# The projections of keys, values and queries on one 128x128 array or on four tiles of 128x32

## The chip, the core and the metric

The kernel runs on one core of a Trainium2 chip. The metric is the time of one execution on the device in microseconds (us), the median of several runs. A profile is of one execution, which has its own time.

## What is computed

The input is `x` of 16 images, 64x64 places, 128 features, all in 32-bit floating point. Layer 0 is a two-dimensional LSTM over each image (each place takes the states of the place above and to the left) after a group norm. Layer 1 is a Nystrom attention with 8 heads of 16 features and 64 landmarks, followed by a recurrent layer over the 4096 places. The change touches the attention alone, of which this is the core (b images, n = 4096 places, h = 8 heads, dh = 16, m = 64 landmarks):

```python
xn = (x - mu) * rsqrt(var + eps) * gamma + beta
q, k, v = split(xn @ w_qkv, 3)             # w_qkv is 128 x 384; then split into heads
q = q * dh ** -0.5
q_l, k_l = mean of q, k over each of the m landmarks' places
attn1 = softmax(q @ k_l.T)                 # n x m
attn2 = softmax(q_l @ k_l.T)               # m x m, then its pseudo-inverse, by 6 iterations
attn3 = softmax(q_l @ k.T)                 # m x n
out = attn1 @ pinv(attn2) @ (attn3 @ v) + convolution of v over 33 places
out = x + out @ w_out + b_out
```

## The kernel before

The program has five stages one after the other: statistics of the images, the LSTM over diagonals (`lstm_grid`), the landmarks with the pseudo-inverse (`landmarks`), the attention (`attention`, from line 845 on), and the recurrent layer (`recurrence`). In the trace the attention goes from some 1611 us to some 3370 us.

**Groups and steps.** The attention cuts the 4096 places of an image into Q = 8 groups of GC = 512 places, so 16 images are 128 groups. Groups go through a pipeline of two images' depth: in step s the group s is projected (`new`); the group s-8 of the image before (`mid`) has its attn3 exponentials and its sums over values; and the groups around s-16 of the image before that (`first`, `cur`, `third`, `fourth`, `fifth`, `sixth`) are finished: attn1, product with the inverse, convolution, output product, and the first product of the recurrent layer. Steps 0 to 7 run `first_step`, 8 to 14 `second_step`, 15 to 127 `step` (lines 1396 to 1484), and what is left `last_step`. A step with s a multiple of 8 has `start` set: the image changes, and between the projections and the next products stand extra ones that close the image before (`gather`, `turn_split`, `spread_values`). Of the 113 runs of `step`, 14 are such (s = 16, 24, ..., 120) and 99 are not.

**What sets the order.** The stage runs under a manual schedule: PE, DVE, ACT and POOL each execute in the order in which `step` calls its helpers; semaphores hold an instruction until its inputs are there and its buffer is free. SP issues the DMAs. PSUM holds eight banks of 128 partitions x 512 floats: `bank0` to `bank5`, and `pair`, which is two banks.

**The products around the change, in PE's order in a usual step.**

- `compare` (L1131): 16 products of 32 rows x 128 columns, four row tiles at a time, into banks 4, 5 and the pair.
- `project_keys` (L979): one product, weights `wqkv[:, 128:256]` (128x128), moving operand `xT` (128x512), into bank 0. ACT copies it to `KT` (L983).
- `project_values` (L989): four products, weights a 128x128 piece of `xT`, moving operand `wqkv[:, 256:384]` (128x128), into bank 1. ACT copies it to `V` (L993), and SP stores that.
- `project_queries` (L999): one product, weights `wqkv[:, 0:128]`, moving `xT`, into bank 5. ACT scales it into `QT` (L1003).
- `greatest` (L1024): four products of 32 rows x 128 columns x 512, into banks 0 to 3, so it needs the copies L983 and L993 done. DVE takes the maxima (L1028).
- `weigh` (L1054, L1060), `output` (L1208), `turn_top` (L1155), `turn_output` (L960 from `at_z`), `attend` (L1180: eight tiles of 64 rows x 32 columns side by side), `convolve` (L1103: the same tile), `feed` (L1240), `turn_rows` (L960 from `at_xh`), `attend_values` (L1076: four tiles of 128 rows x 32 columns side by side, 16 products of 128 columns), and `soften` (L1166, L1168).

A product in 32-bit floats stands in the trace as two passes, each a weight load (LDWEIGHTS, on the row PEld) and a MATMUL (row PE). A tile's rows are set by the partitions of the operands, its columns by the partitions of the output. `quarter(n)` is the slice of partitions 32n to 32n+32.

Of the kernel before, what the change touches and what calls it, by code (L numbers as in the profile page):

```python
# [14 lines left out]
P = 128  # L15
# [830 lines left out]
def attention(nc, tc, t1, gamma, beta, wqkv, ident, mhalf, fixed, xp, rows, qm, km, pinvT, vd, t2, wx, wx_stats, out, ahead):  # L846
# [16 lines left out]
    NP = H // 2  # L863
# [3 lines left out]
    with ExitStack() as ctx:  # L867
# [10 lines left out]
        def banks(*ks):  # L878
            return [bank(k, [P, GC]) for k in ks]
# [94 lines left out]
            gr.zT = wk.tile([P, GC], F32, tag="zT", name="at_zT")  # L974
            nc.scalar.copy(gr.zT, gr.pz)

        def project_keys(gr, p=None):
            gr.pk = banks(0)[0] if p is None else p
            nc.tensor.matmul(gr.pk, wqkv[:, P : 2 * P], gr.xT, start=True, stop=True)  # L979

        def keep_keys(gr):
            gr.KT = kv.tile([P, GC], F32, tag="KT", name="at_KT")
            nc.scalar.copy(gr.KT, gr.pk)  # L983

        def project_values(gr, p=None):
            gr.pv = banks(1)[0] if p is None else p
            for c in range(C):
                cs = slice(c * P, (c + 1) * P)
                nc.tensor.matmul(gr.pv[:, cs], gr.xT[:, cs], wqkv[:, 2 * P : 3 * P], start=True, stop=True)  # L989

        def keep_projected(gr):
            gr.V = kv.tile([P, C, F], F32, tag="V", name="at_v")
            nc.scalar.copy(gr.V.rearrange("p c f -> p (c f)"), gr.pv)  # L993
            rows = vd[gr.im.b, DH + gr.g * GC : DH + (gr.g + 1) * GC, :]
            nc.sync.dma_start(out=rows.rearrange("(k p) f -> p k f", p=P), in_=gr.V)

        def project_queries(gr):
            (gr.pq,) = banks(5)
            nc.tensor.matmul(gr.pq, wqkv[:, 0:P], gr.xT, start=True, stop=True)  # L999

        def keep_queries(gr):
            gr.QT = big.tile([P, GC], F32, tag="QT", name="at_QT", bufs=2 * Q + 1)
            nc.scalar.mul(gr.QT, gr.pq, 0.25)  # L1003

        def turn_split(im):
            r = bank(3, [P, P])
            nc.tensor.transpose(r, split.rearrange("p n s -> p (n s)"), ident)
            im.minus = wk.tile([P, P], BF, tag="minus", name="at_minus3")
            nc.scalar.copy(im.minus, r)
# [10 lines left out]
        def greatest(gr):  # L1020

            gr.s = banks(0, 1, 2, 3)
            for n in range(NP):
                nc.tensor.matmul(gr.s[n], gr.im.qm[quarter(n)], gr.KT[quarter(n)], start=True, stop=True)  # L1024
# [19 lines left out]
        def sums(im):  # L1044
            im.sums = sm.tile([P, P], F32, tag="sums", name="at_sums")
            im.total = wk.tile([P, NP, P], F32, tag="total", name="at_total", bufs=2)
# [24 lines left out]
        def attend_values(gr, k=5):  # L1071

            p = bank(k, [P, P])
            for c in range(C):
                for n in range(NP):
                    nc.tensor.matmul(  # L1076
                        p[quarter(n)], gr.V[:, c, quarter(n)], gr.e[:, n, c, :],
                        start=(c == 0), stop=(c == C - 1), skip_group_check=True,
                    )
            gr.p = p  # L1080

        def keep_values(gr):
            im, p = gr.im, gr.p
            if gr.g == 0:
                nc.vector.tensor_copy(im.sums, p)
            else:
                nc.vector.tensor_tensor(im.sums, p, im.sums, ALU.add)
# [37 lines left out]
        def compare(gr):  # L1125

            gr.both = pair()
            gr.s = (*banks(4, 5), gr.both[:, 0], gr.both[:, 1])
            for c in range(C):
                for n in range(NP):  # L1130
                    nc.tensor.matmul(  # L1131
                        gr.s[n][:, c * P : (c + 1) * P], gr.QT[quarter(n), c * P : (c + 1) * P],
                        gr.im.km[quarter(n)], start=True, stop=True,
                    )

        def topmost(gr):
            gr.mx = sm.tile([P, NP, C, 2], F32, tag="cmx", name="at_cmx")
            for s, n, k in ((gr.s[1], 1, 1), (gr.both.rearrange("p n x -> p (n x)"), 2, 2), (gr.s[0], 0, 1)):
                nc.vector.tensor_reduce(  # L1139
                    gr.mx[:, n : n + k].rearrange("p n c j -> p (n c j)"), s.rearrange("p (x m) -> p x m", m=M), AX.X, ALU.max  # L1140
                )
# [28 lines left out]
        def softened(gr):  # L1170
            gr.eT = wk.tile([P, NP, GC], F32, tag="eT", name="at_eT")
            for n in range(NP):
                nc.scalar.activation(gr.eT[:, n], gr.s[n], AF.Exp)  # L1173
# [42 lines left out]
        def measure(gr, cs=range(C)):  # L1216
            if 0 in cs:
                gr.mu = sm.tile([P, C, 2], F32, tag="mu", name="at_mu")
            for c in cs:
                st = sm.tile([P, 6], F32, tag="st", name="at_st")  # L1220
                nc.vector.bn_stats(st, gr.u[:, c, :])
                nc.vector.bn_aggr(gr.mu[:, c, :], st)
# [24 lines left out]
        def measure_feed(gr):  # L1247
            nc.vector.bn_stats(wx_stats[:, gr.im.b * Q + gr.g, :], gr.fx)
# [3 lines left out]
        def group(s):  # L1252
            b, g = divmod(s, Q)
            return images[b].groups[g] if b in images else None
# [141 lines left out]
        def step(s):  # L1396
            b, q = divmod(s, Q)
            new, after, mid, was = group(s), group(s + 1), group(s - Q), group(s - Q - 1)
            first, cur, third, fourth, fifth, sixth = (group(s - 2 * Q + d) for d in (1, 0, -1, -2, -3, -4))
            start = q == 0  # L1400
            if first:
                compare(first)
            if cur:
                softened(cur)
            project_keys(new)
            if start:
                sums(mid.im)
            project_values(new)
            if s == 2 * Q - 1:
                attend_values(was, 3)  # L1410
                keep_values(was)
            if first:
                topmost(first)
            if sixth:
                measure_feed(sixth)
            if fourth:
                measure(fourth, (0,))
            keep_keys(new)
            keep_projected(new)
            project_queries(new)  # L1420
            if start and was:
                gather(was.im)
            if fourth:
                measure(fourth, (1,))
            keep_queries(new)
            if start:
                turn_split(mid.im)
            if fifth:
                normalise(fifth)
            greatest(new)  # L1430
            if first:
                carry_factors(first)
                carry(first, 2, nc.gpsimd)
            weigh(mid)
            keep_greatest(new)
            if first:
                part_top(first)
            if third:
                output(third)
            weights(mid)  # L1440
            if first:
                carry(first, 3, nc.gpsimd)
            if start and was:
                spread_values(was.im)
            if first:
                turn_top(first)
            if fifth:
                turn_output(fifth)
                keep_output(fifth)
            if third:  # L1450
                keep_sum(third)
            if fourth:
                measure(fourth, (2, 3))
            if cur:
                attend(cur)
            if first:
                keep_top(first)
            add_weights(mid, (3, 1, 0), mid.g == 0)
            if fourth:
                factors(fourth)  # L1460
            add_weights(mid, (2,))
            if q == Q - 1:
                shift(new.im)
            if cur:
                convolve(cur, pair())
                divide(cur)
            if fifth:
                feed(fifth)
            if after:
                turn_rows(after)  # L1470
            if fifth:
                keep_feed(fifth)
            if after:
                keep_rows(after)
            if first:
                carry(first, 0, nc.scalar)
            attend_values(mid)
            if cur:
                add_convolved(cur)
            keep_values(mid)  # L1480
            if first:
                soften(first)
                carry(first, 1, nc.scalar)
                carry_bias(first)
            if cur:
                turn_attended(cur)
            fetch(s)
# [345 lines left out]
```

## Time and profile before

| what | value |
| --- | --- |
| time, median of 3 runs | 3641.82 us (3641.27 to 3644.77) |
| time of the profiled execution | 3638.97 us |
| its span, first to last instruction | 3637.4 us |
| mean granted TensorE clock | 0.991 |
| busy: PE, PEld, DVE, ACT, POOL | 96%, 65%, 82%, 69%, 68% of the span |
| instructions on PE and on PEld | 36874 each |
| a usual step (trace, 2401.41 to 2414.18) | 12.77 us |
| a step that changes the image (trace, 2452.65 to 2468.44) | 15.79 us |

The busy time of PE counts each MATMUL to its modelled end, and MATMULs overlap one another, so PE shows as busy where it only waits for the array to empty. What a product costs in the chain of PE is read from the distance between starts: from its first instruction's start to the start of the next line's.

### The profile page before, as it was taken

How to read it: one execution, taken by the hardware profiler on the slowest of the kernel's cores; microseconds unless marked ns; L12 is line 12 of the kernel's file. 1: busy time of each engine (PE TensorE's matmuls, PEld its weight loads, DVE VectorE, ACT ScalarE, POOL GpSimd, SP SyncE). 2: the span in 40 equal slices, each digit the busy share in tenths (PEclk: the TensorE clock that was granted, in tenths of full speed). 3: DMA queues.
4: the chain of work that ended last, by engine and by line, in shares of the span. 5: the costliest groups of instructions: out<-in, count | busy, mean ns of one | idle time of the engine just before them, and what ended most of it. 6: DMA issues, size and time to landing. Idle time of an engine off the chain costs nothing. (4 is left out here: it accounts for less than half of the span.)

```text
span 3637.4 us, 99065 instructions
## 1 busy us (share of the span) xinstructions
PE 3503.6 (96%) x36874; PEld 2372.5 (65%) x36874; DVE 2987.7 (82%) x7005; ACT 2499.6 (69%) x5126; POOL 2487.0 (68%) x3843
## 2 busy tenths in 40 slices
PE   7899999999999998999999999999999999997988
PEld 6666665545567666975666666666666666654777
DVE  8699999998889887544888888888888888888665
ACT  0466556666667666345788888888888888876787
POOL 1577877777788885325777777777777777785223
PEclk9999999999999999999999999999999999999999
DMA  9223332333333321033777777777676777667799
GB/s 349 76 75 79 81 84 81 83 83 86 87 86 85 80 77 36 4 74 85 165 174 186 166 165 164 163 167 163 161 162 162 162 166 164 157 143 187 199 273 183
DMA packets 834182, 484.04 MB, mean 133 GB/s; under 512 B 304672, under 2 KB 800672, under 8 KB 833696
## 3 DMA queue, kind: packets, MB, share of 16 engines
q1 hardware_dynamic: 814026, 442.55, 47.7%
q0 software_dynamic: 17728, 34.61, 5.3%
q8 instruction: 294, 4.82, 0.6%
q14 instruction: 192, 1.57, 0.1%
q10 hardware_dynamic: 1942, 0.50, 0.1%
HBM read 239.21 MB, written 238.29 MB: 131 GB/s over the span
## 5 line engine op out<-in xcount | busy, mean ns | idle before, releaser
L1096 POOL TENSOR_TENSOR at_total<-at_total,at_e 128x512 f32<-128x512 f32 x472 | 601.4, 1274 | 238.1 <-ACT at_e L1069 218.5
L290 ACT ACTIVATE ls_g<-ls_z,ls_b 128x304 f32<-128x304 f32 (+26 forms) x950 | 493.4, 545 | 222.8 <-PE ls_z L288 190.8
L283 PE MATMUL ls_z<-ls_xn,ls_w 128*128 128x432 f32 (+28 forms) x1700 | 587.4, 493 | 1.5 <-POOL ls_xn L275 1.2
L283 PEld LDWEIGHTS ls_z<-ls_xn,ls_w 128*128 128x128 f32 x1700 | 310.6, 191 | 189.6 <-issue 98.9
L288 PE MATMUL ls_z<-ls_hsum,ls_u 128*128 128x304 f32 (+26 forms) x1140 | 367.9, 459 | 0.0
L1028 DVE TENSOR_REDUCE at_mxq<-at_bank 128x1 f32<-128x512 f32 x512 | 317.7, 682 | 52.8 <-PE at_bank L1024 52.8
L323 POOL TENSOR_TENSOR ls_tt<-ls_ve,mhalf 128x8 f32<-128x8 f32 (+2 forms) x190 | 312.8, 1646 | 18.3 <-DVE ls_ve L322 2.0
L288 PEld LDWEIGHTS ls_z<-ls_hsum,ls_u 128*128 128x128 f32 x1140 | 210.1, 192 | 128.3 <-issue 78.3
L1173 ACT ACTIVATE at_eT<-at_bank 128x512 f32<-128x512 f32 x512 | 264.3, 603 | 41.4 <-PE at_bank L1168 40.8
L406 ACT ACTIVATE ls_g<-ls_cell 128x304 f32<-128x304 f32 (+26 forms) x190 | 93.2, 491 | 268.4 <-DVE ls_cell L405 268.4
L288 PE MATMUL ls_z<-ls_h,ls_u 128*128 128x304 f32 (+26 forms) x760 | 255.4, 459 | 12.3 <-DVE ls_h L410 12.3
L402 POOL TENSOR_TENSOR ls_g<-ls_g,ls_cell 128x304 f32<-128x304 f32 (+26 forms) x190 | 180.4, 949 | 126.6 <-ACT ls_g L290 115.8
L340 ACT ACTIVATE ls_tt<-ls_tt,ls_nb 128x128 f32<-128x128 f32 (+9 forms) x632 | 261.0, 478 | 4.3 <-POOL ls_tt L323 3.4
L275 POOL TENSOR_TENSOR ls_xn<-ls_xn,grstd 128x272 f32<-128x272 f32 (+40 forms) x186 | 209.8, 1128 | 75.1 <-DVE ls_xn L270 66.7
L1139 DVE TENSOR_REDUCE at_cmx<-at_bank 128x8 f32<-128x512 f32 x256 | 175.5, 685 | 104.0 <-PE at_pair L1131 102.4
L1244 ACT COPY at_fx<-at_bank 128x512 f32<-128x512 f32 x128 | 134.1, 1048 | 143.6 <-PE at_bank L1240 138.0
L1615 DVE SCALAR_TENSOR_TENSOR rc_y<-rc_w,rc_scale,rc_z 128x256 f32<-128x256 f32 x344 | 154.5, 480 | 86.2 <-PE rc_z L1602 84.4
L1234 ACT ACTIVATE at_z<-at_u,at_nb,at_r 128x128 f32<-128x128 f32 x512 | 209.6, 484 | 4.6 <-POOL at_nb L1229 4.5
L288 PEld LDWEIGHTS ls_z<-ls_h,ls_u 128*128 128x128 f32 x760 | 141.1, 191 | 106.8 <-issue 52.5
L1596 POOL DMA_DIRECT2D out_dram<-rc_tt x64 | 77.4, 1209 | 168.2 <-ACT rc_tt L1593 147.8
L1189 DVE STREAM_TRANSPOSE at_t<-at_bank 128x512 f32<-128x512 f32 x256 | 167.9, 694 | 28.4 <-PE at_bank L1180 27.3
L1602 PE MATMUL rc_z<-rc_y,rc_vT 128*128 128x256 f32 x688 | 172.9, 392 | 12.5 <-ACT rc_y L1623 11.8
(283 smaller groups left out, 9809.6 us busy)
## 6 DMA issues: line engine op xcount, KB each, us to landing
at_win<-vd SPq DMA_DIRECT2D x256, 256.0 KB
t<-ls_tt SPq DMA_DIRECT2D x392, 130.0 KB
at_T<-t SPq DMA_DIRECT2D x128, 264.0 KB
gs_xb<-in_x_dram SPq DMA_DIRECT2D x64, 512.0 KB
at_xh<-t SPq DMA_DIRECT2D x128, 256.0 KB
vd<-at_v SPq DMA_DIRECT2D x128, 256.0 KB
t<-at_u SPq DMA_DIRECT2D x128, 256.0 KB
out_dram<-at_u SPq DMA_DIRECT2D x128, 256.0 KB
```

Source lines behind the costliest of these rows:

```text
L275: eng.tensor_tensor(a, a, norm(v, grstd), ALU.mult)
L283: nc.tensor.matmul(v.z[g][:, : v.total], wt[g], v.xn[:, : v.total], start=True, stop=True)
L288: nc.tensor.matmul(view(v, v.first.z[g]), ut[g], hin, start=False, stop=True, skip_group_check=True)
L290: nc.scalar.activation(a[:, : v.cols], z, AF.Tanh if g == 4 else AF.Sigmoid, bias=bt[g])
L323: nc.gpsimd.tensor_tensor(v.tt[:, 0:k, F + 2 : F + 4], ve[:, :, :k].rearrange("p r k -> p k r"), mhalf[:, : 2 * k].rearrange("p (k r) -> p ...
L340: nc.scalar.activation(v.tt[:q, k, F + 4 :], v.tt[:q, k, 0:F], AF.Identity, bias=v.nb[:q, k : k + 1], scale=v.tt[:q, k, F + 3 : F + 4],)
L402: nc.gpsimd.tensor_mul(v.a[1], v.a[1], v.cl)
L1028: nc.vector.tensor_reduce(gr.im.mxq[:, n : n + 1, gr.g], gr.s[n], AX.X, ALU.max)
L1096: eng.tensor_tensor(total, total, e[:, :, c, :], ALU.add)
L1139: nc.vector.tensor_reduce(gr.mx[:, n : n + k].rearrange("p n c j -> p (n c j)"), s.rearrange("p (x m) -> p x m", m=M), AX.X, ALU.max)
L1173: nc.scalar.activation(gr.eT[:, n], gr.s[n], AF.Exp)
L1234: nc.scalar.activation(gr.z[:, c, :], gr.u[:, c, :], AF.Identity, bias=gr.nb[:, c : c + 1], scale=gr.r3[:, c : c + 1])
```

## The change

The projections of keys, values and queries get a flag `apart`. With it a product is no longer one of 128 weight columns but four of 32 columns, each into its own quarter of the output's partitions, with the same moving operand. The operands, the banks, the results and the places in the order stay what they are. `step` sets the flag unless the step changes the image; `first_step` and `second_step` do not set it.

```diff
+        def product(out, lhsT, rhs, apart):
+            for r in map(quarter, range(NP)) if apart else (slice(0, P),):
+                nc.tensor.matmul(out[r], lhsT[:, r], rhs, start=True, stop=True)
+
-        def project_keys(gr, p=None):
+        def project_keys(gr, p=None, apart=False):
             gr.pk = banks(0)[0] if p is None else p
-            nc.tensor.matmul(gr.pk, wqkv[:, P : 2 * P], gr.xT, start=True, stop=True)
+            product(gr.pk, wqkv[:, P : 2 * P], gr.xT, apart)
...
-        def project_values(gr, p=None):
+        def project_values(gr, p=None, apart=False):
             gr.pv = banks(1)[0] if p is None else p
             for c in range(C):
                 cs = slice(c * P, (c + 1) * P)
-                nc.tensor.matmul(gr.pv[:, cs], gr.xT[:, cs], wqkv[:, 2 * P : 3 * P], start=True, stop=True)
+                product(gr.pv[:, cs], gr.xT[:, cs], wqkv[:, 2 * P : 3 * P], apart)
...
-        def project_queries(gr):
+        def project_queries(gr, apart=False):
             (gr.pq,) = banks(5)
-            nc.tensor.matmul(gr.pq, wqkv[:, 0:P], gr.xT, start=True, stop=True)
+            product(gr.pq, wqkv[:, 0:P], gr.xT, apart)
...
-            project_keys(new)
+            project_keys(new, apart=not start)
             if start:
                 sums(mid.im)
-            project_values(new)
+            project_values(new, apart=not start)
...
-            project_queries(new)
+            project_queries(new, apart=not start)
```

(`NP` is 4, `P` is 128.) The last three edits are in `step`.

## Prediction

> **What bounds the kernel now.** I read the page first: PE is busy nearly throughout, its clock is granted in full, and every other engine has room.
>
> ```profile
> PE 3503.6 (96%) x36874; PEld 2372.5 (65%) x36874; DVE 2987.7 (82%) x7005; ACT 2499.6 (69%) x5126; POOL 2487.0 (68%) x3843
> ...
> PEclk9999999999999999999999999999999999999999
> ```
>
> A busy PE can still be a waiting PE, so I next took the timeline of PE over one step that is no change of image, from one L979 to the next. Columns: start, length, line, tile (rows*columns), shape, count.
>
> ```profile
> 2401.41 1.13 PE L979 MATMUL at_bank<-at_xT,wqkv 128*128 128x512 f32 x2
> 2402.37 1.05 PE L989 MATMUL at_bank<-wqkv,at_xT 128*128 128x128 f32 x8
> 2403.26 1.02 PE L999 MATMUL at_bank<-at_xT,wqkv 128*128 128x512 f32 x2
> 2404.22 1.14 PE L1024 MATMUL at_bank<-at_KT,qm 32*128 32x512 f32 x8
> ...
> 2408.15 1.09 PE L1180 MATMUL at_bank<-at_eT,at_g 64*32 64x512 f32 x16
> 2409.04 0.64 PE L1103 MATMUL at_pair<-at_win,bands 64*32 64x256 f32 x16
> 2409.60 1.13 PE L1240 MATMUL at_bank<-at_zT,at_wfT 128*128 128x512 f32 x2
> 2410.57 0.60 PE L960 MATMUL at_bank<-ident,at_xh 128*128 128x128 f32 x4
> 2411.10 1.08 PE L1076 MATMUL at_bank<-at_e,at_v 128*32 128x128 f32 x32
> 2412.11 0.40 PE L1166 MATMUL at_bank<-at_topT,at_minus 32*128 32x512 bf16 x4
> ```
>
> Only distances between starts count here. L989 needs 0.89 us for its eight passes of 128 columns. L979 needs 0.96 for two passes of 512 columns, and so does L1240 (0.97): both come straight after another tile shape. L1180 also makes two rounds of 512 columns straight after another shape, but in tiles of 32 columns, and needs 0.89.
>
> Single records of the trace (to the ns, medians of the 98 usual steps s = 17 to 127) tell why. Write E for the first weight load of L979. After the last MATMUL of another shape starts, the next shape's first load comes 0.200 later where that MATMUL has 128 columns: 0.107 for its own streaming and 0.093 in which the array empties. This 0.093 is the same in each direction (L1131 to L979, L960 to L1076, L1076 to L1166, L1060 to L1208). Then the first pass lasts longer than the others, since its weight load has nothing to hide under: L979's first pass takes 0.533 and its second 0.429, so 0.104 of load is bare. With 32 columns the bare load is small: L1180's first round takes 0.454 and its second 0.429; L1076's first 0.134, each later one 0.109. So 0.025 is bare.
>
> Usual steps repeat at 12.77 (12.77 to 12.78 in most, up to 12.93), so one chain sets them. Adding the streaming of a step's 17 groups (107 ns for each 128 columns of a round in f32, 53 in bf16) gives about 11.3; seven changes of shape at some 0.12 to 0.20 and a few ns per pass make the rest. So **PE's own order bounds these steps**, and a piece taken off its chain shortens them.
>
> **The change, part by part.**
>
> *Keys.* Two passes become two rounds of four tiles. In L1076 and L1180 the tiles of a round start 6.7 ns apart (0, 7, 14, 20) and both passes interleave by rounds, so I price a round as they show it: first 0.454, second 0.429, against 0.533 and 0.429. Gain 0.079.
>
> *Values.* Eight passes at 0.1113 on average (0.779 from the first to the last start, 0.112 to L999) become eight rounds at 0.1092, L1076's pace: 0.891 against 0.874. Gain 0.017.
>
> *Queries.* First round 0.429 against 0.431. The last pass now ends with the fourth tile, 0.020 after the first, so the way to L1024's load is 0.020 + 0.427 + 0.093 = 0.540 against 0.521. Loss 0.017. L1024's own first load of 128 columns stays bare as before.
>
> Sum: 2.805 before (0.533 + 0.429 + 0.779 + 0.112 + 0.431 + 0.521), 2.726 after: **0.079 a step**, 0.075 if the array empties as slowly as L1076 to the first MATMUL of L1166 has it (0.205). That saving is a load of 128 columns at the change of shape becoming one of 32; nothing streams faster.
>
> The Trainium skill (TensorE: Matmul & The Clock Gate, LDWEIGHTS) gives a load as its columns over 1.2 GHz, 107 ns for 128 and 27 for 32. The trace's 104 and 25 agree; by the page the sum would be 0.080.
>
> *Instructions.* Six products become 24, so 36 more pairs of load and MATMUL, on 190 in a step. In a round of L1076 four pairs go out in 20 ns, so PE's sequencer can issue them; I take them at nothing beyond the 20 ns above. If that cover is gone, see the second rival.
>
> *Waits.* The change adds none; it lets PE arrive 0.08 earlier, so I looked at what is next in time.
>
> Two rows of the waits (us in total, times, longest):
>
> ```profile
> DVE at_cmx L1139 <- PE at_pair L1131: 102.4, 112, 1.8
> ...
> PEld at_bank L1024 <- ACT at_v L993: 84.8, 112, 0.8
> ```
>
> The second is 0.757 each time and looks like a bound, but the copy L993 ends at E+2.64 and the load goes at E+2.81, just when the array is empty; L993 itself waits for L989, which moves ahead with the rest. The keys' copy L983 is held by ACT (the four L1173 end at E+1.33), so it will not move; it still ends 0.9 before L1024. By the first row DVE starts each step with 0.9 idle, waiting for L1131; then runs without a stop to L1203. It gains little until L1028 (ready some 0.03 before PE's L1024 ends), so DVE will lag PE by up to 0.05 after that. The closest demand on it is bank 5 for L1131: L1087 ends at 2412.83, the load goes at 2412.88, the MATMUL at 2413.195, so the last of its four tiles' loads (2412.896 + 0.107) leaves 0.19, then 0.14. POOL waits 1.87 per step for the exponentials (L1069), which follow PE. No DMA moves in order; the queues carry the same bytes in a step that is 0.6% shorter, at 77% busy in the step above.
>
> *Which steps.* `step` runs 99 times without `start`. In s = 15 PE waits 1.34 before L999 for bank 5, so its gain is lost there; I count 98. In steps that change the image L1007 comes right when POOL has the split ready (L1042 ends 2456.34, load 2456.40); that chain starts from L1069 of the step before, behind the projections, and moves with PE. So all 98 hold: 98 x 0.079 = **7.7 us** (7.4 at 0.075). The profiled execution would take 3638.97 - 7.7 = 3631.3. The runs' median lies 2.85 above that execution; from it, 3641.82 - 7.7 = **3634.1**, 0.21% less. What a measurement of this kernel can tell from no change is about 0.2%, or 7.3 us, so the forecast sits on that line.
>
> **Rivals.**
>
> 1. *A round is dearer because all four tiles read one operand* (slower). In L1076, L1180 and L1131 the tiles of a round stream different data: other columns of `at_e` or `at_eT`, or other partitions. Here four tiles stream the same `xT`, or the same columns of `wqkv`, at the same time, and no row shows that. If the reads stand in each other's way, the 12 rounds' worth of 2.56 us streaming grows; the change loses from 3.1% on (0.079 / 2.56). Two by two would double it: (2.56 - 0.08) x 98 = 243, so 3885 us. For it: nothing but the missing row. Against: the tiles of a round start 6.7 ns apart and read eight streams at once in L1180 without slowing. Chance 0.08.
>
> 2. *Starts cost more than 6.7 ns.* With 25 ns between the tiles of a round, the fourth ends 0.075 after the first instead of 0.020, rounds of 128 columns still hide it (4 x 25 = 100 under 109), and a step gains 0.079 - 0.055 = 0.024: 2.4 us, 3639.5. Against: 6.7 ns in four groups of the step. The Trainium skill (TensorEngine Tiling, Instruction Overhead) gives every matmul some 60 cycles, which is 25 ns at the full clock, and by it this rival would hold; the trace's rows of tiles side by side do not bear it out. Together with other partial losses (a bare load of the next tile, DVE's margin of 0.14 used up): chance 0.10, at 3637 to 3641.
>
> 3. *Hidden anyway*: another engine holds the step at 12.77. For it: the regular length, and DVE's long run. Against: DVE's idle 0.9, POOL's 1.87, and PE's distances, which the shapes alone explain. 3641.8, chance 0.06.
>
> That the change does not do what it says is excluded: the built program has four rows of 32x512 for L979 and 16 of 32x128 for the values in these steps.
>
> **How the numbers follow.** Forecast 0.74, rival 1 0.08, rival 2 0.10, rival 3 0.06, and 0.02 for more than forecast. Within the forecast the medians can differ by 1 to 2 us by chance, and 7.7 is 0.4 beyond the line, so I give 0.44 of its 0.74 to faster and 0.30 to no change. Faster 0.46, same 0.30 + 0.10 + 0.06 - 0.01 = 0.45, slower 0.08 + 0.01 (chance) = 0.09. The range goes from 3631 (the profiled execution's own base) to 3642 (rival 3): it leaves out rival 1 and the tail.
>
> **What would show it.** Right: the distance from L979's first start to L1024's falls from 2.81 to 2.73, L979's first round is 0.454, the values' rounds are 0.109 apart, usual steps repeat at 12.69, steps that change the image stay at 15.79. Wrong: rounds over 0.43 or 0.11 (rival 1), tiles of a round more than 7 ns apart (rival 2), a new idle in front of L1024, L1131 or L1208 with steps still at 12.77 (rival 3), or a longer emptying of the array between L1131 and the keys than 0.093.

## The result, and the profile after

The changed kernel takes 3635.2 us, the median of 22 runs (3628.9 to 3640.0), against 3642.2 us of the kernel before (22 runs beside them, 3636.5 to 3647.3). The ratio is 0.9979, with a 95% interval of 0.9973 to 0.9985, which is 5.5 to 9.8 us less.

In the changed kernel the lines behind the new helper stand 4 further down, and all three projections are recorded at the helper's line, L979. L1024 of before is L1028, L1131 is L1135, and so on. The page first:

```profile
span 3636.9 us, 106193 instructions
...
PE 3499.9 (96%) x40438; PEld 2343.7 (64%) x40438; DVE 2982.8 (82%) x7005; ACT 2499.9 (69%) x5126; POOL 2489.2 (68%) x3843
...
PEclk9999999999999999999999999999999999999999
```

The page has 3564 more MATMULs (36 a step in 99 steps: 18 products more, of two passes each), nearly the same shares, and a span only 0.5 us shorter than before's. The page can't show the gain, so I took the timeline of PE over one usual step (start, length, line, tile, shape, count):

```profile
2406.92 1.06 PE L979 MATMUL at_bank<-at_xT,wqkv 128*32 128x512 f32 x8
2407.80 1.06 PE L979 MATMUL at_bank<-wqkv,at_xT 128*32 128x128 f32 x32
2408.68 1.04 PE L979 MATMUL at_bank<-at_xT,wqkv 128*32 128x512 f32 x8
2409.65 1.14 PE L1028 MATMUL at_bank<-at_KT,qm 32*128 32x512 f32 x8
```

Keys now take 0.88 from start to start instead of 0.96, values 0.88 instead of 0.89, queries 0.97 instead of 0.96. From the first start of the keys to L1028 it is 2.73 where it was 2.81. The windows of two steps in a row, cut at the first start of the keys (columns: window, length, busy time of PE, PEld, DVE, ACT and POOL with counts, granted clock, DMA share, GB/s), show that the whole step keeps this gain:

```profile
2406.92:2419.61 12.69, 12.69 (x226) 8.15 (x222) 11.32 (x24) 10.66 (x22) 10.10 (x17) 1.00 0.75 170
2419.61:2432.30 12.69, 12.69 (x226) 8.23 (x222) 11.32 (x24) 10.63 (x22) 10.10 (x17) 1.00 0.72 167
```

The single records, as medians over the 98 usual steps (us; "to L1028" is L1024 before):

| | before | after | predicted |
| --- | --- | --- | --- |
| last start of L1131 (L1135 after) to the keys' first start | 0.200 | 0.200 | 0.200 |
| keys, first round | 0.533 | 0.453 | 0.454 |
| keys, second round, to the values | 0.429 | 0.429 | 0.429 |
| values, first start to that of the queries | 0.891 | 0.873 | 0.874 |
| queries, first round | 0.431 | 0.429 | 0.429 |
| queries, first to fourth tile's start | 0 | 0.020 | 0.020 |
| last start to L1028's load | 0.521 | 0.521 | 0.520 |
| keys' start to L1028's load | 2.805 | 2.726 | 2.726 |
| a usual step | 12.774 | 12.694 | 12.69 |
| eight steps, one change of image among them | 105.208 | 104.653 | |

Eight steps lose 0.555, which is seven times 0.079: the eighth, where the image changes, lost nothing. From L1028 of step 17 to that of step 127 the stretch is 7.45 us shorter (1436.82 against 1444.27). Three usual steps in it gained nothing: those that begin at L1028 of s = 41, 45 and 49 last 12.93 in both kernels. In them DVE starts its maxima (L1032) some 0.35 later than in step 42, and PE stands longer in front of L1212 than there, by 0.15 (by 0.07 in front of L1208 before).

**Why the span hides it.** In these two profiled executions the stages ahead of the attention, whose code is the same, took 6.7 us longer after than before (the first L1028 came at 1622.5 against 1615.8), and steps 14 to 17 took 40.79 against 38.74. In both places the clock record has stretches at half clock. The windows around step 15 in the profile of after (column before the DMA share: granted clock):

```profile
1705.00:1715.00 10.00, 8.11 (x120) 5.77 (x112) 1.76 (x3) 2.65 (x5) 6.93 (x8) 0.66 0.07 19
1715.00:1735.00 20.00, 16.49 (x250) 11.42 (x246) 11.11 (x20) 11.68 (x24) 12.07 (x26) 1.00 0.17 48
1735.00:1739.00 4.00, 4.00 (x68) 2.28 (x52) 2.96 (x5) 1.50 (x4) 2.90 (x3) 0.57 0.21 49
```

PE idles 1.9 us of the first window, 1.4 and 0.5 just ahead of 1708.2 while it waits for the exponentials (L1073); from 1707.9 to 1714.8 the clock is granted at half, and again for most of the third window. Before had one such piece there, from 1701.6 to 1705.0. The whole span had 75.5 us at half clock after, and 65.3 before. The seventh experiment, further down, has the same step 15 and one short piece there, so the changed code of that step does not by itself make the stretch longer. One execution's whole time says little about a change of 8 us; the distances inside the steps, all at full clock, say it to some ns.

### The profile page after: what moved, and what is told of

Its sections match the earlier page's. It is cut to its first block, busy times and chain, and to the rows that moved or that the text cites. A ratio compares the mean times of both kernels' runs of the same rounds, so it can differ in the third digit from the quotient of the medians.

```text
span 3636.9 us, 106193 instructions
## 1 busy us (share of the span) xinstructions
PE 3499.9 (96%) x40438; PEld 2343.7 (64%) x40438; DVE 2982.8 (82%) x7005; ACT 2499.9 (69%) x5126; POOL 2489.2 (68%) x3843
## 5 line engine op out<-in xcount | busy, mean ns | idle before, releaser
L1032 DVE TENSOR_REDUCE at_mxq<-at_bank 128x1 f32<-128x512 f32 x512 | 314.9, 677 | 53.0 <-PE at_bank L1028 53.0
L979 PE MATMUL at_bank<-at_xT,wqkv 128*32 128x512 f32 (+1 forms) x1684 | 262.8, 602 | 2.0 <-DVE at_cmx L1143 1.1
```

Source lines behind the costliest of these rows:

```text
L979: nc.tensor.matmul(out[r], lhsT[:, r], rhs, start=True, stop=True)
L1032: nc.vector.tensor_reduce(gr.im.mxq[:, n : n + 1, gr.g], gr.s[n], AX.X, ALU.max)
```

## The experiments

The theory: the time saved in a usual step is the keys' first weight load, bare at the change of tile shape, which has 32 columns instead of 128; the price is the skew of the four tiles at the end. The rivals: (a) the tiles stream faster or overlap more than one product does, so that each projection saves something by itself; (b) only the keys matter, and the other two could stay as they were; and, for the order of the tiles, that it does not matter in which order their passes are written. All edits are made on the changed kernel.

**Experiments 1 and 2: keys alone, and keys with values.** The rest goes back to one product of 128 columns.

```diff
 # experiment 1
-            project_values(new, apart=not start)
+            project_values(new)
...
-            project_queries(new, apart=not start)
+            project_queries(new)
 # experiment 2: only the second of these
```

> Only the keys are four tiles; values and queries are whole again. Theory (each change of tile shape costs the emptying of the array, 0.093 us, plus a bare weight load, 0.104 for 128 columns and 0.025 for 32; nothing else changes): against the kernel before, the keys gain 0.079, and a new change of shape in front of the values costs 0.020 + 0.093 + 0.104 - 0.002 = 0.215, so a usual step is 0.136 longer, 12.91 us, and the run 13.3 us longer (ratio 1.0037). Rival a (the tiles themselves make a product cheaper, each product keeps its own share): the step is shorter than before, 12.69 to 12.75. Rival b (it is the earlier copy of the keys on ACT that helps): the same gain as the full change, 12.69.

> Keys and values are four tiles, queries whole. Theory: against before the keys gain 0.079, the values 0.015, and the change of shape now stands in front of the queries: 0.020 + 0.093 + 0.104 more there. A usual step is 0.118 to 0.122 longer, 12.89 us, the run some 11.7 us longer (ratio 1.0032). Rival a: 12.68 to 12.70, nearly the whole gain of the change, since the values are the largest part. Rival b: 12.69.

Measured: 3652.97 us for keys alone, ratio to the kernel before 1.0035 (1.0023 to 1.0047), and 3652.08 us for keys and values, 1.0029 (1.0020 to 1.0038). Usual steps repeat at 12.913 and 12.893, as expected. The timelines, keys alone first:

```profile
2408.82 1.07 PE L979 MATMUL at_bank<-at_xT,wqkv 128*32 128x512 f32 x8
2409.82 1.16 PE L979 MATMUL at_bank<-wqkv,at_xT 128*128 128x128 f32 x8
2410.81 1.02 PE L979 MATMUL at_bank<-at_xT,wqkv 128*128 128x512 f32 x2
2411.76 1.14 PE L1028 MATMUL at_bank<-at_KT,qm 32*128 32x512 f32 x8
```

```profile
2410.25 1.06 PE L979 MATMUL at_bank<-at_xT,wqkv 128*32 128x512 f32 x8
2411.13 1.06 PE L979 MATMUL at_bank<-wqkv,at_xT 128*32 128x128 f32 x32
2412.12 1.12 PE L979 MATMUL at_bank<-at_xT,wqkv 128*128 128x512 f32 x2
2413.18 1.14 PE L1028 MATMUL at_bank<-at_KT,qm 32*128 32x512 f32 x8
```

With keys alone the way from the keys to the values is 1.00 (0.88 in the full change) and that of the values 0.99, of which the single records put 0.104 on the values' first round: the bare load of 128 columns has moved from the keys to the values. With keys and values it has moved on to the queries: 0.99 from the values to them, and their first round is 0.533. In each, a new change of shape costs what the old one cost (emptying plus bare load), and the keys' round is still the 0.453 of the full change. So rivals (a) and (b) fall: no projection gains more for itself than the 0.018 of the values' rounds, and of the sets of projections that were run only the whole of what stands between one change of shape and the next makes the step shorter.

**Experiment 3: two tiles of 64 columns.**

```diff
-            for r in map(quarter, range(NP)) if apart else (slice(0, P),):
+            for r in map(half, range(2)) if apart else (slice(0, P),):
```

> Two tiles of 64 columns in place of four of 32 in the same steps. Theory (the bare load goes with the columns): about half of 0.104 stays bare, 0.052; first round 0.481 in place of 0.533; the values' rounds at some 0.110; the skew at the end 0.007. A usual step is 0.059 shorter than before, 12.715 us, the run 5.8 us shorter (ratio 0.9984). Rival c (what matters is that the tile is the one that other products of the step use, 32 columns): no gain, 12.77. Rival d (any split takes the whole load away): 12.69.

Measured: 3636.55 us, ratio 0.9988 (0.9979 to 0.9997); usual steps at 12.707.

```profile
2401.79 1.08 PE L979 MATMUL at_bank<-at_xT,wqkv 128*64 128x512 f32 x4
2402.70 1.04 PE L979 MATMUL at_bank<-wqkv,at_xT 128*64 128x128 f32 x16
2403.57 1.03 PE L979 MATMUL at_bank<-at_xT,wqkv 128*64 128x512 f32 x4
2404.53 1.14 PE L1028 MATMUL at_bank<-at_KT,qm 32*128 32x512 f32 x8
```

The keys' first round is 0.480, so the bare load is 0.051: 0.104, 0.051 and 0.025 for 128, 64 and 32 columns, in proportion. The skew is 0.007 instead of 0.020. The step gained 0.067 where 0.059 was expected: I had put the values' rounds halfway, and they take 0.109, as with 32 columns. The theory holds in size as well as in sign.

**Experiment 4: the passes of the values written tile by tile.** Same products; all four pieces of `xT` for the first quarter of columns, then for the second, and so on.

```diff
-            for c in range(C):
-                cs = slice(c * P, (c + 1) * P)
-                product(gr.pv[:, cs], gr.xT[:, cs], wqkv[:, 2 * P : 3 * P], apart)
+            for r in map(quarter, range(NP)) if apart else (slice(0, P),):
+                for c in range(C):
+                    x = gr.xT[:, c * P : (c + 1) * P]
+                    nc.tensor.matmul(
+                        gr.pv[r, c * P : (c + 1) * P], x[:, r], wqkv[:, 2 * P : 3 * P], start=True, stop=True
+                    )
```

> As the change, but the values' 16 products are written tile by tile: the four pieces of one tile one after the other, then the next tile, so neighbours in PE's order use the same tile. Theory (PE starts its passes in the order written, and only neighbours on different tiles overlap): the values lose their rounds, up to 32 passes of 0.107 us = 3.4 us in place of 0.87, at best some overlap where tiles meet; a usual step of 15 us, up to 250 us more in all. Rival e (PE finds passes for free tiles by itself, whatever the order): 12.69 us a step as in the change.

Measured: 3768.56 us in one run; a step 14.073, that is 1.38 more than in the change. The values are L994 here, L1031 is the L1028 of the change.

```profile
2422.05 1.06 PE L979 MATMUL at_bank<-at_xT,wqkv 128*32 128x512 f32 x8
2422.93 2.11 PE L994 MATMUL at_bank<-wqkv,at_xT 128*32 128x128 f32 x29
2424.78 0.63 PE L979 MATMUL at_bank<-at_xT,wqkv 128*32 128x512 f32 x3
2424.88 0.49 PE L994 MATMUL at_bank<-wqkv,at_xT 128*32 128x128 f32 x3
2425.21 1.02 PE L979 MATMUL at_bank<-at_xT,wqkv 128*32 128x512 f32 x5
2426.16 1.14 PE L1031 MATMUL at_bank<-at_KT,qm 32*128 32x512 f32 x8
```

The order does matter, but my expectation of up to 15 was for tiles strictly one after the other, and they are not. A tile has eight passes; the single records show the next tile's first pass beginning as the fifth of the tile before it begins (2423.371 and 2423.377). So about two tiles run at any time, and the queries' first tiles (third row) start before the values' last tile is done. The expectation had room for some overlap where tiles meet, but neither side of it had two tiles running beside one another all along.

**Experiment 5: the values in pairs of pieces.** Now a tile has four passes in a row before the next tile's are written.

```diff
-            for c in range(C):
-                cs = slice(c * P, (c + 1) * P)
-                product(gr.pv[:, cs], gr.xT[:, cs], wqkv[:, 2 * P : 3 * P], apart)
+            for c0 in range(0, C, 2):
+                for r in map(quarter, range(NP)) if apart else (slice(0, P),):
+                    for c in (c0, c0 + 1):
+                        x = gr.xT[:, c * P : (c + 1) * P]
+                        nc.tensor.matmul(
+                            gr.pv[r, c * P : (c + 1) * P], x[:, r], wqkv[:, 2 * P : 3 * P], start=True, stop=True
+                        )
```

> As e4, but a tile gets only two neighbouring products (four passes) before the next tile's. In e4 the next tile began when the fifth of a tile's eight passes began, so I now hold that PE hands passes out in the order written, each tile taking one that runs and three that wait. By that, four passes of a tile all fit, the next tile starts some 7 ns later, and a usual step is 12.69 us again. Rival (only direct neighbours on different tiles overlap): half of e4's loss or so stays, 13.1 to 13.5 us. Rival (room for fewer waiting passes): 12.8 to 13.4 us.

Measured: 3645.46 us in one run (3646.04 for the kernel before beside it); a step 12.747, 0.053 more than in the change. The values are L995 here, and L1032 is the L1028 of the change.

```profile
2419.55 1.06 PE L979 MATMUL at_bank<-at_xT,wqkv 128*32 128x512 f32 x8
2420.44 1.11 PE L995 MATMUL at_bank<-wqkv,at_xT 128*32 128x128 f32 x32
2421.31 1.09 PE L979 MATMUL at_bank<-at_xT,wqkv 128*32 128x512 f32 x8
2422.33 1.14 PE L1032 MATMUL at_bank<-at_KT,qm 32*128 32x512 f32 x8
```

Four passes of one tile in a row do not hold the next tile back: the values take 0.87 again, and the four tiles run beside one another. What is left is the skew, 0.073 at the queries' end instead of 0.020: it comes in with the values, where the second to fourth tile start late and have a bare first load (their first pass takes 0.133 instead of 0.109). After one pass the skew is 0.056, and the second pair of pieces brings it to 0.073. The expectation of 12.69 missed this 0.053. Experiments 4 and 5 fit a picture in which passes are handed out in the written order and a tile holds one that runs and three that wait; a fifth holds up all that is written behind it. That picture is argued from these two runs. No run varies the count between four and eight.

**Experiment 6: the split in the steps that change the image, too.**

```diff
-            project_keys(new, apart=not start)
+            project_keys(new, apart=True)
```

(and the same for values and queries).

> The flag is set in the steps that change the image too. Usual steps 12.69 us as in the change. By PE's order alone a step that changes the image gains 0.096 for keys and values, and loses 0.217 where the queries' tiles give way to the whole transposes of gather (0.020 + 0.093 + 0.104): 0.12 more, so eight steps take 104.77 us in place of 104.65, and the run 1.7 us more than the change. Rival (in that step PE waits for POOL's split, about 0.11 us in front of L1007, which hides the loss): eight steps 104.65 to 104.67 us.

Measured: 3643.2 us in one run; usual steps 12.694 as in the change, but eight steps 104.720 against 104.653, so a step that changes the image is 0.067 longer. In such a step L1116, L1118 and L1011, products on the whole array, come between the queries and L1028. The timeline from the queries on, experiment 6 and then the change:

```profile
2458.23 1.04 PE L979 MATMUL at_bank<-at_xT,wqkv 128*32 128x512 f32 x8
2459.20 0.33 PE L1116 MATMUL at_bank<-ident,at_sums 128*128 128x128 f32 x1
2459.37 0.95 PE L1118 MATMUL at_bank<-at_ones,at_total 128*128 128x2 f32 x8
2460.26 0.33 PE L1011 MATMUL at_bank<-ident,at_split 128*128 128x128 f32 x1
```

```profile
2459.70 1.02 PE L979 MATMUL at_bank<-at_xT,wqkv 128*128 128x512 f32 x2
2460.56 0.27 PE L1116 MATMUL at_bank<-ident,at_sums 128*128 128x128 f32 x1
2460.67 0.95 PE L1118 MATMUL at_bank<-at_ones,at_total 128*128 128x2 f32 x8
2461.60 0.33 PE L1011 MATMUL at_bank<-ident,at_split 128*128 128x128 f32 x1
```

With the split, keys and values gain 0.080 and 0.018 as in a usual step, but L1116 comes 0.97 after the queries instead of 0.86, since the array has to empty in front of it, and its first pass takes 0.166 instead of 0.109. Its load, a transposing one of a single pass, is bare for 0.057, not for the 0.104 that I had put into PE's order. The wait for POOL ahead of L1011 swallows 0.04 of the loss (0.187 instead of 0.228), and 0.04 is lost again in L1028, whose third and fourth tile start 0.665 after the first instead of 0.625; what holds them there is not shown. The result lies between the two expectations: PE's order alone said 104.77, POOL as the bound 104.65 to 104.67. To leave these steps out, as the change does, is worth 0.067 x 14 = 0.9 us.

**Experiment 7: the split of keys and values in `second_step` (steps 8 to 14).** There PE waits much, and the other engines set the steps.

```diff
-            project_keys(new)
+            project_keys(new, apart=True)
...
-            project_values(new)
+            project_values(new, apart=True)
```

> The change, and keys and values as tiles in the seven second steps too, where attend_values with the same tile comes right behind them. By PE's order alone a step gains 0.079 + 0.017 + 0.122 for the change of shape that falls away, 0.218 us, so the first 14 steps take 79.1 us in place of 80.63. Rival, which I hold: these steps repeat at 7.55 us by the chain from the exponentials (L1069, 2.2 us) to POOL's sums of them (5.3 us) and back, through the one buffer that they share; PE's gain is hidden and the 14 steps take 80.4 to 80.63 us.

Measured: 3633.9 us in one run; steps 0 to 14 take 80.70 against 80.63 in the change and before. By PE's order they would have come down to 79.1. The waits in 1620 to 1700 us (who waits for whom: us in total, times, longest) name what holds them:

```profile
ACT at_e L1073 <- POOL at_total L1100: 9.2, 4, 2.3
```

The row is the same in the change but for its total, 9.1: ACT's exponentials wait 2.3 a step for POOL to add up those before, and what PE gains does not shorten the steps. In this run step 15 is the same code as in the change, and its steps 14 to 17 took 38.31, with one short piece at half clock:

```profile
1708.00:1712.00 4.00, 4.00 (x64) 2.71 (x68) 0.00 (x0) 0.50 (x1) 3.77 (x4) 0.63 0.01 2
1712.00:1735.00 23.00, 19.04 (x306) 12.99 (x298) 12.42 (x22) 11.99 (x25) 16.03 (x32) 1.00 0.16 42
```

So the longer step 15 in the profile of after is a matter of that execution. Over the profiles the stretch goes with the pieces at half clock in it: with one of 3.4 us steps 14 to 17 took 38.3 to 38.7 (before, experiments 3 and 7), with two 39.4 (experiment 6), with one of 6.8 and one of 3.4 they took 40.7 to 41.1 (after, experiments 1, 2 and 5). Experiment 4, whose steps are longer themselves, is left out of this.

No experiment gave a kernel that measurably beats the change.

## Why the prediction was right, step by step

- **Keys: right.** First round 0.453 against 0.454 forecast, a gain of 0.080. Experiments 1 to 3 show the cause: the bare load follows the columns (0.104, 0.051, 0.025) and moves to where the change of shape is put.
- **Values: right.** 0.873 against 0.874. The small gain is the rounds' pace, 0.109 instead of 0.111. That two tiles keep the same pace as four (experiment 3) speaks against an overlap that grows with the tiles.
- **Queries: right.** The way out to the load is 0.020 + 0.521 = 0.541 against 0.540; with the first round, shorter by 0.002, that is a loss of 0.018 against 0.017. The loss is the skew: when experiment 5 widened it to 0.073, the step grew by the same 0.053.
- **Sum: right.** 0.079 from the keys' start to L1028's load and 0.080 in the length of the step, against 0.079; over eight steps 0.555 = 7 x 0.079. That all 98 steps hold was wrong for three, which stayed at 12.93; they cost 0.24 of the 7.7 us. The medians fell by 7.0 us and the ratio by 0.21%; 7.7 us and 0.21% were forecast.
- **Rival 1 (one shared operand is dearer) falls.** Rounds of 512 columns take 0.429 and of 128 columns 0.109 with all four tiles reading one operand, as in the groups where they read different ones.
- **Rival 2 (starts cost more) falls.** The tiles of a round start 6.7 ns apart. This is also where the Trainium skill's 60 cycles for each matmul (TensorEngine Tiling, Instruction Overhead) do not hold for tiles side by side.
- **Rival 3 (hidden anyway) falls for usual steps**, which repeat at 12.694. It is true of the three steps of 12.93, and of steps 8 to 14, as experiment 7 shows.
- **Steps that change the image: right.** They stayed as they were.
- **DVE's margin: the term that was mis-sized.** I let DVE lag PE by up to 0.05 more and the margin in front of bank 5 fall from 0.19 to 0.14. In the step from 2406.92, L1091's copy ends at 2418.257, the last of the four loads is at 2418.324 and lasts 0.107, and the MATMUL is at 2418.625: 0.19, as before. DVE moved with PE as a whole, and its wait for L1135, the second row here, stayed as long as it was. Before, the three rows had 218.5, 102.4 and 84.8:

```profile
POOL at_total L1100 <- ACT at_e L1073: 208.6, 112, 3.0
...
DVE at_cmx L1143 <- PE at_pair L1135: 102.1, 111, 1.8
...
PEld at_bank L1028 <- ACT at_v L997: 92.8, 112, 0.8
```

The last row grew by 8.0, about the whole gain, and still bounds nothing: it counts the time in which the load stands behind a copy (L997) that ends 0.134 before the load goes (0.167 before the change). By this row alone a reader would take ACT for the new bound; the step's length shows that it isn't.

- **Step 15: right in that no gain was seen there**, and not in that it would be unchanged: its length goes with the pieces of half clock that fall into it.
- **The base.** Both ways of counting, 3631.3 from the profiled execution and 3634.1 from the median, were 7.7 less than their base; the second is the one that met the median. Executions of one kernel spread over 11 us here, more than the gain, so the single profiled time was no base for the forecast.

## What to carry to other kernels

Where PE's own order sets a step, look at the first weight load after each change of tile shape. Here nothing hid it, it cost in proportion to its columns (0.104, 0.051 and 0.025 us for 128, 64 and 32), and it was made smaller by giving the whole run of neighbouring products the narrow shape. Splitting one product of the run only moves the bare load to the next, and loses (ratio 1.0035 for keys alone, 0.9979 for all three). Write the tiles' passes alternately, and judge a gain of 0.2% by distances inside steps in the trace and by many runs, not by one profile's span.

## What the runs showed of the hardware that I had not expected

- Tiles side by side do not run freely: written tile by tile with eight passes each, about two of four overlap (a step 14.07 instead of 12.69 us); with four passes each, all four do (12.75).
- The bare load of a product of 128x128 is not one number: 0.104 for f32 weights loaded in two passes, 0.057 for the one-pass product with `ident` in L1116.
- The granted clock falls to half for pieces of 3.41 us or a multiple (but for the last piece, which runs into the end of the record), in step 15 at 1707.9, when PE had idled for some 1.6 of the 3.4 us before it, and where they fall differs between executions: 65 to 89 us at half clock in the nine profiles, whatever the kernel. The Trainium skill (TensorE: Matmul & The Clock Gate, Part 1) gives a free-running window of 3413 ns and half the clock after an idle one, and the length of the pieces agrees; that a window must be idle throughout is not what step 15 shows, where four passes stand between the two idle times (1.38 and 0.50).
